# A four-stage block kernel on one core: lanes, PSUM banks and attention bursts regrouped

## The chip, the core and the metric

The kernel runs on one core of a Trainium2 chip. The metric is device time in microseconds (us) for one execution, from three runs; the profile is one further execution, taken by the hardware profiler. Engines are named as in the profile: PE (TensorE matmul), PEld (its weight load), DVE (VectorE), ACT (ScalarE), POOL (GpSimd), SP (SyncE, which issues the DMAs).

## What is computed

The input is x of 8 batches x 512 rows x 128 numbers, all float32. Four blocks follow each other, each with a residual:

```
x = x + gelu(linear_attention(layernorm(x)))        # 16 heads of 64: 1024 channels
x = x + fp4_ffn(layernorm(x))                       # 128 -> 352 -> 128, blocks of 16 quantised
x = x + causal_attention(layernorm(x))              # 16 heads of 8
x = x + experts(rmsnorm(layernorm(x)))              # 8 experts, best two, low-rank updates
```

The first block is per channel: with Q = elu(q)+1 and K = elu(k)+1,

```
KV = sum_s K*v;  Ksum = sum_s K;  out = (Q * KV / (Q*Ksum + 1e-6)) @ wo + bo
```

so each of the 1024 channels needs a reciprocal at each of 512 positions. The second block quantises its inputs, its weights and its middle to FP4 in groups of 16. The fourth computes both chosen experts of a token by masking the low-rank parts.

## The kernel before

Batches are independent. Each passes four functions: `linear_attention` (lines 650-698), `fp4_feed_forward` (747-791), `causal_attention` (794-929), then `routed` and `experts` (934-1058).

**The planner.** The functions issue nothing themselves. Each call becomes a `Step` of a `Plan` (129-307), with an engine, a cost (`cost`, 365-400) and the steps that it needs. `Plan.ordered` (221-297) replays all steps on five engines in its own time: at each moment an engine takes, among the steps that are ready and whose buffers are free, the one of lowest rank. `Plan.issue` (299-307) then emits them in that order, so every instruction of the main part has line 307 in the profile, and groups are told apart by tile names. On the chip each engine keeps that order and waits where an operand is late. Ranks come from `plan.span(lane, low, high)` (1061-1076), which spreads the steps of a function over an interval, in units of one batch. A lane hands out the places of a tag in the order of its own steps. `one_go` makes several calls one step.

**The lanes.** There are three: "front" runs linear attention of batch b at ranks b-1.0 to b-0.4 and the FP4 block at b-0.4 to b; "attention" runs at b to b+1; "experts" at b+1 to b+2.

**PSUM.** Eight banks: two `pair` tiles of two banks each for attention scores, one `mid` bank for the rest of attention, two `ahead` banks for the matmuls of the linear, FP4 and expert stages, and one `asum` bank for their accumulations (declared at 494-497; taken at lines 652, 776, 1036, 1046). `linear_attention` takes `asum` before its first chunk and holds it until its eighth.

**Linear attention**, eight chunks of 128 channels. A chunk has three 128x512 matmuls (q, k, v), five evictions by ACT, one DVE pass over q and k together (128x1024), two `scalar_tensor_tensor` for elu+1, one for K*v with its sum, one reciprocal of 128x512, one POOL product and one output matmul into `asum` (lines 653-686).

**Causal attention**, four groups of four heads. `spread` copies eight rows per head by nine DMAs into one of three K/Q tile pairs. `maxima` computes scores once for the row maxima (matmuls of 32 rows, four heads side by side on the array, then DVE `tensor_reduce`), and sends the maxima back by a DMA as a ninth row of Q. `scores` computes them again transposed, ACT takes the exponential, POOL masks the diagonal block. `weighed` multiplies by V, 32 columns per head, and `divided` normalises. Within a batch the maxima of group g+1 stand ahead of the scores of group g; nothing of batch b+1 is begun inside batch b.

Of the kernel before, what the change touches and what calls it, by code (L numbers as in the profile page):

```python
# [9 lines left out]
F32 = mybir.dt.float32  # L10
# [21 lines left out]
NFM = FM // P  # L32
NEG = -1.0e30
# [95 lines left out]
class Plan:  # L129
# [3 lines left out]
    HOP = {"tensor": 0.25, "vector": 0.12, "scalar": 0.12, "gpsimd": 0.15, "sync": 2.2}  # L133
# [38 lines left out]
    def one_go(self):  # L172
        return OneGo(self)

# [46 lines left out]
    def ordered(self):  # L221
# [25 lines left out]
        while done < len(self.steps):  # L247
            for e in self.engines:
                while busy[e] <= now:
# [19 lines left out]
                    s.start, s.end = now, now + s.cost  # L269
                    busy[e] = now + (0.06 if e == "sync" else s.cost)  # L270
# [54 lines left out]

class Span:
# [38 lines left out]
def cost(engine, method, out, ins, a, k):  # L365
# [3 lines left out]
    if engine == "tensor":  # L369
        if method == "transpose":  # L370
            return 0.14
        lhs, rhs = (list(a) + [k.get("lhsT"), k.get("rhs")])[1:3]
        rows, cols = lhs.shape[0], _free(lhs)
        n = _free(rhs)
        if BF16 in (getattr(lhs, "dtype", None), getattr(rhs, "dtype", None)):
            return 0.1
        if rows == 32:
            return 0.02 + n * 0.71e-3
        if cols == 32:
            return 0.02 + n * 0.8e-3  # L380
        return max(0.2, n * 1.667e-3)
    if engine == "vector":
        if method == "reciprocal":
            return 0.06 + n * 6.42e-3
        if method == "tensor_scalar":
            return 0.17 + n * 0.6e-3
        if method == "bn_stats":
            return 0.28
        return 0.15 + wide * 1.05e-3
    if engine == "scalar":  # L390
        return 0.25 + wide * 0.83e-3
    if engine == "gpsimd":
        if method == "affine_select":
            return 0.2 + n * 0.9e-3
        if method == "memset":
            return 0.15
        if k.get("op") == ALU.pow or ALU.pow in a:
            return 1.02
        return 0.12 + n * 2.25e-3
    return 2.0  # L400


LANES = ("front", "attention", "experts")
# [8 lines left out]
    ("xn", [P, NT, D], 2, F32),  # L412
    ("xnT", [P, S], 2, F32),
    ("two", [P, 2, S], 4, F32),
    ("v", [P, S], 2, F32),
    ("z", [P, S], 2, F32),
    ("wk_o", [P, D], 2, F32),
    ("half", [P, 512], 2, F32),
    ("sc", [P, 44], 4, F32),
    ("qa", [P, 704], 3, F32),  # L420
# [8 lines left out]
    ("oT", [P, NT, P], 1, F32),  # L429
    ("mx", [P, NT, 4], 3, F32),  # L430
    ("mr", [4, S], 1, F32),
# [12 lines left out]
    ("am", [P, 2, S], 1, F32),  # L444
# [4 lines left out]
def block_kernel(  # L449
# [46 lines left out]
    places("ahead", [P, 512], 2, pool=sums)  # L496
    places("asum", [P, 512], 1, pool=sums)
# [75 lines left out]
    va = const.tile([P, NT, H1, 32], F32, name="va", tag="va")  # L573
    dev.gpsimd.memset(va, 0.0)
    dev.gpsimd.memset(va[:, :, :, 8:9], 1.0)
# [8 lines left out]
    none = const.tile([4, S], F32, name="none", tag="none")  # L584
    dev.gpsimd.memset(none, 0.0)
# [5 lines left out]
    va = plan.fixed(va)  # L591
# [4 lines left out]
    one_go, new = plan.one_go, plan.tile  # L596
# [53 lines left out]
    def linear_attention(b):  # L650
        xnT = normed_T(xs[b], "ahead", "xn", "xnT")
        po = new("asum", [P, S])
        for c in range(NC0):
            cols = ts(c, P)

            ex = new("two", [P, 2, S])
            fm = new("two", [P, 2, S])
            v = new("v", [P, S])
            for i, w in enumerate((wq_sb, wk_sb, wv_sb)):
                pw = new("ahead", [P, S])  # L660
                nc.tensor.matmul(pw, w[:, cols], xnT, start=True, stop=True)
                if i == 2:
                    nc.scalar.activation(
                        v, pw, AF.Identity, bias=bqkv_sb[:, 2, c : c + 1]
                    )
                    break
                nc.scalar.activation(ex[:, i, :], pw, AF.Exp, bias=bqkv_sb[:, i, c : c + 1])
                nc.scalar.activation(
                    fm[:, i, :], pw, AF.Identity, bias=bqk1_sb[:, i, c : c + 1]
                )  # L670
            nc.vector.tensor_scalar(ex, ex, -1.0, 1.0, ALU.add, ALU.add)
            ks = new("s1", [P, 1])
            kv = new("s1", [P, 1])
            kf, qf = fm[:, 1, :], fm[:, 0, :]
            nc.vector.scalar_tensor_tensor(
                kf, ex[:, 1, :], 1.0, kf, ALU.min, ALU.max, accum_out=ks
            )
            nc.vector.scalar_tensor_tensor(qf, ex[:, 0, :], 1.0, qf, ALU.min, ALU.max)
# [3 lines left out]
            nc.vector.reciprocal(z, z)  # L682
            nc.gpsimd.tensor_tensor(z, qf, z, ALU.mult)
            wk_o = new("wk_o", [P, D])
            nc.scalar.activation(wk_o, wo_sb[:, c, :], AF.Copy, scale=kv)
            nc.tensor.matmul(po, wk_o, z, start=(c == 0), stop=(c == NC0 - 1))

        y = new("v", [P, S])
        nc.scalar.activation(y, po, AF.Identity, bias=bo_sb)
# [57 lines left out]
    def fp4_feed_forward(b):  # L747
        xn = new("xn", [P, NT, D])
        ln_apply(xn, xs[b], *ln_stats(xs[b]))
        xq = new("xn", [P, NT, D])  # L750
# [3 lines left out]
        xqT = new("xnT", [P, S])  # L754
        nc.scalar.copy(xqT, transposed(xq, NT, "ahead"))
        hqs = []
        for half in range(2):
            h = new("h", [P, 2, FF])
            for j in range(2):
                t = 2 * half + j  # L760
                pgu = [new("ahead", [P, FF]) for _ in range(2)]
                for i in range(2):
                    nc.tensor.matmul(
                        pgu[i], xqT[:, ts(t, P)],
                        wT[:, i].rearrange("p c m -> p (c m)")[:, 0:FF],
                        start=True, stop=True,
                    )
# [7 lines left out]
            hqs.append(hq)  # L775
        pd = new("asum", [P, NT, D])
        for t in range(NT):
            hqT = new("hqT", [P, NF0, P])
            nc.scalar.copy(
                hqT.rearrange("p c m -> p (c m)"),  # L780
                transposed(
                    hqs[t // 2][:, t % 2, :].rearrange("p (c m) -> p c m", c=NF0), NF0, "ahead"
                ),
            )
            with one_go():
                for c in range(NF0):
                    nc.tensor.matmul(
                        pd[:, t, :], hqT[:, c, :], wT[:, 2, c, :],
                        start=(c == 0), stop=(c == NF0 - 1),
                    )  # L790
        nc.vector.tensor_tensor(xs[b], pd, xs[b], ALU.add)


    def causal_attention(b):
# [7 lines left out]

        def spread(g):
            nc.sync.dma_start(qTs[g % NKT][8:P:32, :], none)
            for i, dst in enumerate((qTs[g % NKT], kTs[g % NKT])):
                for j in range(4):
                    nc.sync.dma_start(
                        dst[32 * j : 32 * j + 8, :],
                        qk[32 * g + 8 * j : 32 * g + 8 * j + 8, i, :],
                    )  # L810

        spread(0)
        spread(1)
        pv = new("mid", [P, S])
        with one_go():
# [5 lines left out]
            va.rearrange("p t h c -> p (t h) c")[:, :, 0:8],  # L821
            pv.rearrange("p (k c) -> p k c", c=8),
        )
        on = new("on", [P, NT, D])

        def largest(g, t, mx):

            n = (t + 1) * P
            pscs = [new("pair", [P, 2, 512]) for _ in range(2)]
            with one_go():  # L830
                for j in range(4):
                    rows = slice(32 * j, 32 * j + 32)
                    nc.tensor.matmul(
                        pscs[j // 2][:, j % 2, 0:n], qTs[g % NKT][rows, ts(t, P)],
                        kTs[g % NKT][rows, 0:n], start=True, stop=False,
# [6 lines left out]
            for i, psc in enumerate(pscs):  # L842
                nc.vector.tensor_reduce(
                    mx[:, t, 2 * i : 2 * i + 2], psc[:, :, 0:n], AX.X, ALU.max, negate=True
                )

        def to_queries(g, mx):

            pt = new("mid", [P, S])
            with one_go():  # L850
                for t in range(NT):
                    nc.tensor.transpose(pt[0:4, ts(t, P)], mx[:, t, :], ident)
            mr = new("mr", [4, S])
            nc.scalar.copy(mr, pt[0:4, :])
            nc.sync.dma_start(qTs[g % NKT][8:P:32, :], mr)

        def scores(g, t):

            n = S - t * P
            pscs = [new("pair", [P, 2, 512]) for _ in range(2)]  # L860
            with one_go():
                for j in range(4):
                    rows = slice(32 * j, 32 * j + 32)
                    nc.tensor.matmul(
                        pscs[j // 2][:, j % 2, 0:n], kTs[g % NKT][rows, ts(t, P)],
                        qTs[g % NKT][rows, t * P : S], start=True, stop=True,
                    )
            prs = []
            for psc in pscs:
                pr = new("pr", [P, 2, S])  # L870
                nc.scalar.activation(pr[:, :, 0:n], psc[:, :, 0:n], AF.Exp, scale=8.0 ** -0.5)

                nc.gpsimd.affine_select(
                    out=pr[:, :, 0:P], in_=pr[:, :, 0:P], pattern=[[0, 2], [1, P]],
                    compare_op=ALU.is_ge, fill=0.0, base=0, channel_multiplier=-1,
                )
                prs.append(pr)
            return prs

        def weighed(g, t, prs, po):  # L880
            with one_go():
                for j in range(4):
                    nc.tensor.matmul(
                        po[32 * j : 32 * j + 32, t * P : S], va[:, t, 4 * g + j, :],
                        prs[j // 2][:, j % 2, 0 : S - t * P],
                        start=(t == 0), stop=(t == NT - 1),
                    )

        def divided(g, po):
            oT = new("oT", [P, NT, P])  # L890
            nc.scalar.copy(oT.rearrange("p t q -> p (t q)"), po)
# [251 lines left out]
```

## Time and profile before

| what | value |
|---|---|
| runs | 1412.92, 1408.03, 1406.41 us; median 1408.03 us |
| profiled execution | 1418.83 us, of which the span of instructions is 1417.0 us |
| PE | busy 1185.3 us (84% of the span), granted clock 0.919 on average |
| DVE | busy 945.6 us (67%) |
| ACT | busy 699.3 us (49%) |
| POOL | busy 561.0 us (40%) |
| DMA | 15.11 MB in all, 6 tenths busy in the first fortieth of the span, below one tenth after |

The span is read in three parts. The first 263 us fill the lanes. From 263 to 1204 us the same pattern returns every 156 to 158 us, once a batch. The last 213 us empty the lanes. The page gives each engine's share in forty slices; a query over chosen stretches gives exact sums, and one over waits tells which engine's event ended an idle time. A float32 matmul that is no transpose leaves two records.

### The profile page before, as it was taken

The numbers are of one execution on the slowest core, as the hardware profiler recorded it, in microseconds if no ns is written. First come the engines' busy times: TensorE is split into PE (matmuls) and PEld (weight loads), VectorE is DVE, ScalarE is ACT, GpSimd is POOL, SyncE is SP. The second block draws the span as 40 slices with busy tenths as digits, with TensorE's granted clock in tenths as the row PEclk, the third lists the DMA queues.
The fourth block names the chain that finished last, engine by engine and source line by source line (L and its number), as shares of the span: only waits on it lengthen the run. The fifth ranks groups of instructions, "written<-read, shape, count | busy, mean of one in ns | idle before, by whom it ended". The sixth has DMA issues, their size and how long they took to land.

```text
span 1417.0 us, 17315 instructions
## 1 busy us (share of the span) xinstructions
PE 1185.3 (84%) x6185; PEld 535.4 (38%) x6185; DVE 945.6 (67%) x1717; ACT 699.3 (49%) x1244; POOL 561.0 (40%) x660
## 2 busy tenths in 40 slices
PE   2626779879998899989998899979998899699867
PEld 0203323433344334533354334433354335344333
DVE  5973894589676877498667976597749866352231
ACT  2632744474547464665547364656447453423321
POOL 3223212422663147423653156514652356244125
PEclk9965986999999899999999999999999999899879
DMA  6000000000000000000000000000000000000000
GB/s 181 0 0 1 12 1 5 2 12 1 5 16 7 7 5 1 17 12 1 6 16 11 2 5 2 9 12 5 2 9 12 1 5 9 6 7 13 1 0 8
DMA packets 18886, 15.11 MB, mean 11 GB/s; under 512 B 3632, under 2 KB 15344, under 8 KB 18800
## 3 DMA queue, kind: packets, MB, share of 16 engines
q1 hardware_dynamic: 18800, 14.01, 4.0%
q8 instruction: 49, 0.80, 0.2%
q14 instruction: 37, 0.30, 0.1%
HBM read 7.18 MB, written 2.10 MB: 7 GB/s over the span
## 4 chain that ended last, share of the span: by engine, by line
PE 47%; DVE 25%; POOL 9%; ACT 7%; issue 4%; POOLq 0%; ACTq 0%; DVEq 0%
PE ahead L307 19%; PE pair L307 13%; PE asum L307 8%; DVE z L307 6%; PE mid L307 6%; DVE mx L307 4%; DVE two L307 3%; DVE qa L307 3%; DVE sc L307 2%; POOL qa L307 2%; ACT pr L307 2%; POOL act L307 2%; POOL hq L307 1%; ACT two L307 1%; POOL z L307 1%
## 5 line engine op out<-in xcount | busy, mean ns | idle before, releaser
L307 DVE TENSOR_REDUCE mx<-pair 128x2 f32<-128x256 f32 (+3 forms) x256 | 198.7, 811 | 78.6 <-PE pair L307 77.8
L307 POOL TENSOR_TENSOR z<-two,z 128x512 f32<-128x512 f32 x64 | 86.4, 1350 | 346.0 <-DVE z L307 289.9
L307 ACT ACTIVATE pr<-pair 128x1024 f32<-128x1024 f32 (+3 forms) x256 | 168.5, 699 | 108.0 <-PE pair L307 103.5
L307 DVE RECIPROCAL z<-z 128x512 f32<-128x512 f32 x64 | 214.1, 3345 | 7.2 <-ACT z L307 7.2
L307 POOL TENSOR_SCALAR_AFFINE_SELECT pr<-pr 128x256 f32<-128x256 f32 x256 | 110.7, 446 | 120.9 <-ACT pr L307 119.4
L307 PE MATMUL pair<-kT,qT 32*128 32x128 f32 (+3 forms) x1024 | 131.6, 503 | 22.5 <-DVE mx L307 22.4
L307 POOL TENSOR_TENSOR act<-act,half 128x512 f32<-128x512 f32 x64 | 81.8, 1279 | 149.0 <-ACT half L307 90.0
L307 PE MATMUL pair<-qT,kT 32*128 32x512 f32 (+3 forms) x1024 | 130.3, 507 | 5.2 <-DVE mx L307 2.5
L307 PE MATMUL ahead<-um,b_sb 128*128 128x512 f32 x256 | 131.5, 614 | 2.9 <-DVE act L307 1.4
L307 ACT ACTIVATE two<-ahead,bqkv_sb 128x512 f32<-128x512 f32 x128 | 87.7, 686 | 59.0 <-PE ahead L307 57.7
L307 PE MATMUL asum<-z,wk_o 128*128 128x512 f32 x128 | 78.9, 702 | 42.6 <-POOL z L307 42.3
L307 PE MATMUL mid<-pr,va 128*32 128x512 f32 (+3 forms) x1024 | 107.5, 462 | 6.9 <-POOL pr L307 4.8
L307 DVE SCALAR_TENSOR_TENSOR two<-two,two 128x512 f32<-128x512 f32 x128 | 105.4, 845 | 3.7 <-DVE two L307 0.5
L307 ACT ACTIVATE two<-ahead,bqk_sb 128x512 f32<-128x512 f32 x128 | 85.7, 683 | 29.6 <-POOL z L307 16.6
L307 ACT ACTIVATE half<-ahead 128x512 f32<-128x512 f32 (+1 forms) x96 | 53.0, 553 | 82.4 <-PE ahead L307 80.5
L307 PEld LDWEIGHTS pair<-kT,qT 32*128 32x128 f32 x1024 | 53.2, 190 | 105.2 <-DVE mx L307 66.2
L307 PE MATMUL ahead<-xnT,wv_sb 128*128 128x512 f32 x128 | 76.5, 682 | 16.1 <-ACT two L307 15.3
L307 DVE SCALAR_TENSOR_TENSOR act<-act,ahead 128x512 f32<-128x512 f32 x64 | 43.3, 677 | 61.3 <-ACT act L307 61.3
L307 POOL TENSOR_TENSOR act<-act,tw 128x512 f32<-128x512 f32 x64 | 81.9, 1279 | 3.2
L307 PEld LDWEIGHTS pair<-qT,kT 32*128 32x128 f32 x1024 | 50.5, 192 | 81.4 <-ACT pr L307 38.3
L307 PE MATMUL ahead<-tT,w_sb 128*128 128x512 f32 x128 | 71.9, 644 | 7.6 <-ACT half L307 5.9
L307 PE MATMUL ahead<-xnT,wq_sb 128*128 128x512 f32 x128 | 72.3, 648 | 6.7 <-ACT half L307 3.4
(163 smaller groups left out, 1957.1 us busy)
## 6 DMA issues: line engine op xcount, KB each, us to landing
x<-in SPq DMA_DIRECT2D x8, 256.0 KB
qT<-qk SPq DMA_DIRECT2D x128, 16.0 KB
kT<-qk SPq DMA_DIRECT2D x128, 16.0 KB
out<-x SPq DMA_DIRECT2D x8, 256.0 KB
w_sb<-in SPq DMA_DIRECT2D x3, 256.0 KB
wq_sb<-in SPq DMA_DIRECT2D x1, 512.0 KB
wk_sb<-in SPq DMA_DIRECT2D x1, 512.0 KB
wv_sb<-in SPq DMA_DIRECT2D x1, 512.0 KB
```

The costliest lines, as they stand in the source:

```text
L307: getattr(e, method)(*a, **k)
```

## The change

1. **Four lanes.** "front" becomes "linear" (ranks b-1.5 to b-0.9) and "fp4" (b-0.9 to b-0.5), each with tiles of its own (`xf`, `xfT` for fp4). Attention of batch b runs at b to b+1, experts at b+1 to b+2, loads at b-2.0.
2. **Three `ahead` banks, no `asum`.** All accumulations take an `ahead` bank. The output projection of linear attention is done in two bursts of four matmuls, one after chunks 0-3 and one after chunks 4-7; the sum of the two goes through `y`. The same for the FP4 down projection and the experts' last matmuls, in two halves of two row tiles. `together` gives the first matmul of a burst the needs of all of them.
3. **Linear attention regrouped.** k, v, q instead of q, k, v; the 128x1024 pass becomes two of 128x512; the reciprocal two of 128x256; the POOL product is written into `qf`, of which there are six.
4. **Attention continued.** Groups are numbered 0 to 31 through all batches; `begin(n+1)` (projection and spread where a batch starts, then maxima) stands ahead of `attended(n)`, over the end of a batch too. V is held twice, at 16 columns per head instead of 32. The zeros that clear Q's ninth row are read from a Q tile instead of a tile of their own. The nine DMAs of a spread are one step.
5. **The planner's costs** are reset, as the third piece of the diff shows for matmuls: lower for the attention's narrow matmuls, nearly the same for the wide ones.

```diff
-LANES = ("front", "attention", "experts")
+LANES = ("linear", "fp4", "attention", "experts")
...
-    places("ahead", [P, 512], 2, pool=sums)
-    places("asum", [P, 512], 1, pool=sums)
+    places("ahead", [P, 512], 3, pool=sums)
...
+class Together:
...
+    def __exit__(self, *_):
+        some = self.plan.steps[self.first :]
+        for s in some[1:]:
+            for n in s.needs:
+                if n not in some:
+                    some[0].needs[n] = True
...
         if rows == 32:
-            return 0.02 + n * 0.71e-3
-        if cols == 32:
-            return 0.02 + n * 0.8e-3
-        return max(0.2, n * 1.667e-3)
+            return 0.068 + n * 0.38e-3
+        if cols < 64:
+            return 0.035 + n * 0.42e-3
+        return 0.03 + n * 1.62e-3
...
+        def feature(c, i, w, tag, **accum):
+            pw = new("ahead", [P, S])
+            nc.tensor.matmul(pw, w[:, ts(c, P)], xnT, start=True, stop=True)
+            ex, f = new("ex", [P, S]), new(tag, [P, S])
+            nc.scalar.activation(ex, pw, AF.Exp, bias=bqkv_sb[:, i, c : c + 1])
+            nc.scalar.activation(f, pw, AF.Identity, bias=bqk1_sb[:, i, c : c + 1])
+            nc.vector.tensor_scalar(ex, ex, -1.0, 1.0, ALU.add, ALU.add)
+            nc.vector.scalar_tensor_tensor(f, ex, 1.0, f, ALU.min, ALU.max, **accum)
+            return f
...
-            nc.vector.reciprocal(z, z)
-            nc.gpsimd.tensor_tensor(z, qf, z, ALU.mult)
+            for part in (slice(0, 256), slice(256, S)):
+                nc.vector.reciprocal(z[:, part], z[:, part])
+            nc.gpsimd.tensor_tensor(qf, qf, z, ALU.mult)
             wk_o = new("wk_o", [P, D])
             nc.scalar.activation(wk_o, wo_sb[:, c, :], AF.Copy, scale=kv)
-            nc.tensor.matmul(po, wk_o, z, start=(c == 0), stop=(c == NC0 - 1))
...
+        for half in range(2):
+            pairs = [products(c) for c in range(4 * half, 4 * half + 4)]
+            po = new("ahead", [P, S])
+            with together():
+                for i, (wk_o, qz) in enumerate(pairs):
+                    nc.tensor.matmul(po, wk_o, qz, start=(i == 0), stop=(i == 3))
+            if half == 0:
+                nc.scalar.activation(y, po, AF.Identity, bias=bo_sb)
+            else:
+                nc.vector.tensor_tensor(y, po, y, ALU.add)
...
+    def begin(n):
+        if n % NG == 0:
+            projected(n // NG)
+            spread(n)
+        if n % NG < NG - 1:
+            spread(n + 1)
+        maxima(n)
+
+    def causal_attention(b):
+        on = new("on", [P, NT, D])
+        for n in range(NG * b, NG * b + NG):
+            if n + 1 < NG * NB:
+                begin(n + 1)
+            attended(n, on)
+        to_model(b, on)
...
-        with plan.span("front", b - 1.0, b - 0.4):
+        with plan.span("linear", b - 1.5, b - 0.9):
             linear_attention(b)
...
-        with plan.span("front", b - 0.4, b):
+        with plan.span("fp4", b - 0.9, b - 0.5):
             fp4_feed_forward(b)
```

The changed program's order can be read without running it, and the prediction uses it. It has the same matmuls, 3689 in all and 460 per batch in mid-run. Before, the first and the last q/k/v matmul of a batch stand 222 matmuls apart on PE, the first and last of the FP4 block 127; after, 359 and 183. Ahead of the first matmul of attention stand 29 q/k/v matmuls before (24 belong to a batch) and 48 after. Behind the last one of the FP4 block stand 475 matmuls before and 574 after.

## The prediction

> **What bounds the kernel now.** I read the forty slices first, then busy sums over stretches cut where the slices change, then the chain and the waits of one batch.
>
> ```profile
> PE   2626779879998899989998899979998899699867
> DVE  5973894589676877498667976597749866352231
> PEclk9965986999999899999999999999999999899879
> ```
>
> PE and DVE swap roles: where DVE shows 8 or 9, PE drops to 6 to 8. The same by stretch (length, then busy us of each engine):
>
> ```profile
> core 0: us, PE busy (x) PEld busy (x) DVE busy (x) ACT busy (x) POOL busy (x), PEclk, DMA share, GB/s
> 0.00:142.00 142.00, 65.18 (x142) 28.12 (x143) 91.48 (x148) 50.70 (x90) 41.30 (x61) 0.77 0.15 45
> 142.00:263.00 121.00, 99.48 (x470) 39.94 (x468) 91.30 (x147) 60.33 (x106) 30.27 (x36) 0.84 0.03 5
> 602.00:655.00 53.00, 44.15 (x193) 20.09 (x191) 48.55 (x84) 27.71 (x49) 12.00 (x9) 0.90 0.05 9
> 655.00:759.00 104.00, 98.68 (x581) 45.41 (x580) 66.64 (x127) 58.16 (x106) 55.85 (x69) 0.97 0.03 8
> 1204.00:1240.00 36.00, 24.79 (x157) 13.70 (x156) 14.30 (x59) 14.70 (x28) 9.85 (x15) 0.82 0.03 6
> 1311.00:1346.00 35.00, 29.67 (x199) 11.59 (x196) 7.79 (x14) 12.74 (x20) 6.52 (x17) 0.80 0.00 1
> ```
>
> 602 to 759 is one batch in mid-run: 53 us in which DVE is 92% busy, then 104 us in which PE is 95% busy and DVE 64%. The chain names the first part's work: the reciprocal, and then what stands behind it.
>
> ```profile
> 605.06 3.26 DVE z L307
> 608.55 1.75 DVE two L307 x3
> 612.11 3.12 issue
> ```
>
> Busy PE is not dense PE, because a matmul's record lengthens when it is fed slowly. So I price work by rows without gaps. Elsewhere in the chain,
>
> ```profile
> 553.83 3.45 PE asum L307 x8
> ```
>
> is four 128x512 matmuls (two records each), 0.86 us each. Likewise, from the timeline at 691 to 705 us: four side-by-side score matmuls of 512, 384, 256, 128 columns 1.14, 0.93, 0.71, 0.50; four V matmuls 1.06, 0.85, 0.64, 0.42; four masks 0.40; a transpose 0.15; a two-pass 128-column matmul 0.22; 352 columns 0.60. Per batch: 68 wide ones 58.7, eight of 352 4.8, scores twice 26.2, masks 6.4, V 11.9, 76 transposes 11.4, 40 two-pass 8.6, the rest 1.0; sum **129 us of PE work**. By the same prices the 53 us hold 36.8 (0.69 per us), the 104 us 91.9 (0.88). DVE has 115 to 118 us per batch. Neither fills 157: the loss is that they are full in turn.
>
> **The change, part by part**, against the profiled execution (1418.83; span 1417.0).
>
> *Lanes and order.* Linear attention is the DVE-heavy part: per chunk 3.35 reciprocal, 0.78, two at 0.85, 0.71, 6.5 us, 52 per batch. Its q/k/v matmuls spread over 222 of a batch's 460 matmuls before, 359 after, so its DVE work lies beside more PE work. What holds it together before is the buffers: `asum` held for eight chunks, and both `ahead` banks held by the experts through two passes. What rate follows? An interpolation between the two stretches would say none is gained; but each is a limit of one engine, and in the middle neither need bind. Evidence from between: ten slices of 17.7 us have DVE at 82 to 90%; they hold 0.72 to 0.95, mean 0.83, several of them on the seam and at half clock. The best PE-bound stretches (503 to 602, 1126 to 1204) hold 0.91. I take the middle, 0.87: **129/0.87 = 148 us per batch** against 156; bounds 0.83 (155) and 0.92 (140).
>
> *What DVE is given.* Two 128x512 passes instead of one of 1024: 0.43 to 0.49 each against 0.78, +0.1 to +0.2, 1.2 per batch. Reciprocal in halves: rows of 44 and 512 elements (427 and 3345 ns) give 6.2 ns per element and 150 ns fixed, so 2 x 1.75 against 3.35, +0.15, 1.2 per batch. One sum for the second burst 0.69, two residuals in halves +0.3. Together +3.4.
>
> *POOL beside DVE.*
>
> ```profile
> L307 DVE SCALAR_TENSOR_TENSOR two<-two,two 128x512 f32<-128x512 f32 x128 | 105.4, 845 | 3.7 <-DVE two L307 0.5
> L307 DVE SCALAR_TENSOR_TENSOR act<-act,ahead 128x512 f32<-128x512 f32 x64 | 43.3, 677 | 61.3 <-ACT act L307 61.3
> ```
>
> The same operation of the same size takes 845 ns with two SBUF inputs and 677 with one from PSUM. The Trainium skill ("SBUF — State Buffer", Who interferes with whom) says why this speaks against the change: a DVE instruction with two SBUF inputs and a POOL one that reads SBUF exclude each other for the whole instruction. By that rule alone each of the five such DVE operations of a chunk (two passes, two elu, K*v) could wait up to a POOL product, 1.28 us: 40 x 1.28 = 51 us per batch, and DVE at 171 would be the bound. By the row the delay today is 0.17 on an elu, 0.10 on the pass, 0.03 on K*v, 3.7 us per batch, with POOL 23% busy in the DVE stretch; spread out it meets POOL's mean of 43%, so about 1.9 times that: +3.3. I take the row. DVE: 116.5+3.4+3.3 = 123 of 148, 83%: it fits.
>
> *The clock.* PE ran at 0.90 in the 53 us, though no wait of PE there exceeds 1.8 us. The skill's rule ("TensorE: Matmul & The Clock Gate", Why this matters for your kernels) is that idle gaps over about 3 us cost the full rate. By the rule nothing is recovered in this stretch; by the row 10% of 53, some 5 us per batch, could be. The 0.87 already has part of it; the rest goes into the range.
>
> *Attention over batch ends.* The 18 spread DMAs of a batch start go out on SP at 0.62 us each (timeline, 607 to 619 us), and the batch's first maxima wait for them. After, they are issued inside the previous batch. As nine in one step they hold SP for 5.6 us, and a DMA of maxima rows that is queued behind, with the scores of its group on PE, waits up to that; loads and stores too, but these have a batch of slack. Between 5.6 us lost per group and 3 gained per batch I take zero, because the maxima run a whole group ahead of the scores. V matmuls of 16 columns stream as many columns: cost zero, weight loads 109 ns beside PE. A zero row read from a Q tile: the same DMA.
>
> *Bursts.* Output matmuls keep number and price. Today PE waits 42.3 us in 26 waits for the POOL product:
>
> ```profile
> PE asum L307 <- POOL z L307: 42.3, 26, 4.6
> DVE x L307 <- PE asum L307: 78.6, 14, 9.1
> ```
>
> A burst waits for its latest input, and all of PE's queue stands behind it; the planner puts it late, so I count the wait at its present sum, between zero and three times that.
>
> *The ends.* In 0 to 142 us DVE is idle for 50 us, 35 of them between 71 and 142, while the FP4 block of batch 0 runs alone. After, 48 instead of 29 q/k/v matmuls stand ahead of the first attention, nearly all of batch 1, whose 52 us of DVE fill this; I take 26 saved (10 to 40). At the end, 1204 to 1240 holds 17.3 us of PE work in 36 and 1311 to 1346 20.3 in 35. After, attention 6 and experts 6 lie beside these parts (574 instead of 475 matmuls follow the last FP4 one); at 0.87 they would take 20 and 23: 28 saved, less a little, 24 (5 to 40). The last experts (1346 to 1417) stay alone.
>
> **Sum.** 263 to 1204 is 6.03 batches of 156: 6.03 x 8 = 48. 48+26+24 = 98; 1418.8-98 = 1321 for the profiled execution, which stood 1.0077 over the median: **1311 us**.
>
> **Rivals.**
> - *Only the ends gain.* The two engines interlock through PSUM (a bank is freed by ACT or DVE, the next matmul waits), the batch stays at 155 to 156. For it: still eight banks, and the seam slices' 0.83. Against it: 0.91 beside DVE at 65 to 67%. 1418.8-50-6 = 1363, median 1353; with half of that at the ends, 1380. Chance 0.24.
> - *Both fill.* 0.92 and ends at their best: 16 x 6.03+80 = 176, median 1233. Chance 0.08.
> - *Slower: PE stands at the bursts.* In the 16 projection bursts PE waits for the fourth pair, which hangs on DVE halves, ACT and a 1.35 us POOL product. Each wait costs itself, and the clock drops behind it. To eat 98 us beyond the 42 present, 16 bursts must wait 8.8 us each; at 12 us it is +52, median 1459. Against it: four pairs take DVE some 26 us and the planner sees that. Chance 0.12.
> - *The order does nothing:* on the chip other waits bring back the old pattern; within 0.5%, 1408. Chance 0.04.
>
> The forecast itself: 0.52. Faster by over 0.5% (about what a measurement of this kernel can tell from no change) 0.52+0.08+0.23 = 0.83; within it 0.05, one part of the first rival with the last; slower 0.12. The range runs from 1250 (0.91 in mid-run and ends near their best) to 1400, just inside the first rival's poor end.
>
> **What would show it.** A batch of 146 to 151 us in mid-run; DVE between 75 and 90% in nearly all slices between the sixth and the thirtieth, without a 9 beside a PE 7; the granted clock over 0.94 on average; attention of batch 0 begun with batch 1's q/k/v done; elu passes at 0.9 to 1.1 us (if they come to 1.5, the port rule was the right one); waits of PE for `qf` under 60 us in all. I am wrong if DVE's rows lengthen with POOL, or if PE's waits move from one end of the burst to the other.

## The result and the profile after

The changed kernel takes 1445.5 us (median; 1442.7 to 1450.6) against 1409.0 for the kernel before on the same chip: ratio 1.026, interval 1.022 to 1.030. It is slower; 1311 was foretold. Its profiled execution took 1450.6 us with a span of 1448.9 and a granted clock of 0.890 (before: 1418.8, 1417.0, 0.919). The main part's line is now L311.

The forty slices of the changed kernel:

```profile
PE   2545778978899799897997889898898889889967
DVE  5879878887856787875976769768975967234231
PEclk9767878989899899996998979999999879989978
```

The swap of roles that the prediction set out from is gone: no long 9 of DVE beside a PE 6 in mid-run. But PE has not become full. A few 7s, and 6s and 7s of the clock, are spread over the run. The same over stretches (columns as in the prediction's table; 585 to 754 us is one batch, 814 to 924 most of another):

```profile
0.00:142.00 142.00, 65.69 (x121) 25.23 (x121) 111.73 (x210) 61.70 (x112) 40.03 (x60) 0.79 0.15 45
142.00:261.00 119.00, 93.56 (x416) 46.34 (x417) 100.42 (x164) 58.97 (x109) 33.18 (x35) 0.81 0.03 5
...
585.00:754.00 169.00, 148.69 (x773) 68.60 (x772) 127.31 (x231) 86.07 (x155) 72.28 (x78) 0.90 0.03 7
...
814.00:867.00 53.00, 41.38 (x236) 18.35 (x229) 34.49 (x94) 22.73 (x45) 15.39 (x21) 0.77 0.06 15
867.00:924.00 57.00, 55.84 (x332) 24.43 (x331) 45.82 (x69) 34.94 (x65) 33.34 (x37) 1.00 0.01 2
```

In 814 to 867 no engine is full: PE 78%, DVE 65%, clock 0.77. Right behind it PE is 98% busy at full clock beside a DVE at 80%. So the two engines can be busy side by side; something else opens holes.

To set the two runs side by side I price each matmul as the prediction does, at the time that it takes without gaps, and note when the same amount of this dense PE work is done (116, 890 and all 1033 us of it). 116 to 890 are six batches, called mid-run from here on. The table has the length of each part in us; the foretold parts are rounded:

| | to 116 | 116 to 890 | per batch | rest | end |
|---|---|---|---|---|---|
| before | 263 | 936 | 156 | 218 | 1417 |
| after | 261 | 990 | 165 | 198 | 1449 |
| foretold | 237 | 888 | 148 | 194 | 1321 |

The 936 us hold 844.6 of busy PE and 91 of idle PE; the 990 hold 877.2 and 113. So of the 54 lost, 21 are longer waits, and 33 go to the *same matmuls taking longer*. The clock tells where: 68 us of the 936 ran at half clock (a granted clock of 0.50), 164 of the 990. In these stretches PE was busy for 141.5 us over 70.1 us of dense work (before: 64.8 over 35.2); in the rest of mid-run it was busy for 736.5 us over 703.9 (before: 779.4 over 739.0), which is less stretched than before.

Five of the waits of PE and DVE in the changed kernel (us in total, times, longest):

```profile
PE ahead L311 <- POOL qf L311: 24.3, 8, 5.4
PE pair L311 <- DMA kT<-qk: 22.4, 18, 6.9
DVE st linear L311 <- DMA x<-in: 21.9, 4, 6.7
PE mid L311 <- DVE on L311: 18.0, 7, 4.8
PE ahead L311 <- DVE act L311: 14.4, 6, 4.5
```

and before, where no wait of PE's matmuls for a `kT` DMA is listed, only two of its weight loads:

```profile
PEld pair L307 <- DMA kT<-qk: 1.5, 2, 0.8
DVE st front L307 <- DMA x<-in: 3.8, 1, 3.8
PE mid L307 <- DVE on L307: 5.3, 9, 1.1
PE ahead L307 <- DVE act L307: 1.9, 3, 0.9
```

The bursts (`qf`) are no trouble: 24 us against 42 before, of which mid-run has 1.1 against 19.6. Two of the other four name a DMA. The timeline at one of the three late x loads (start, length, engine, operation):

```profile
816.37 0.38 SPq L311 DMA_DIRECT2D out<-x  x1
...
817.63 0.54 SPq L311 DMA_DIRECT2D qT<-qT  x1
...
818.22 2.66 SPq L311 DMA_DIRECT2D qT<-qk  x4
...
820.92 2.63 SPq L311 DMA_DIRECT2D kT<-qk  x4
...
823.60 0.44 SPq L311 DMA_DIRECT2D x<-in  x1
826.35 0.68 DVE L311 BATCH_NORM_STATS2 st linear<-x 128x6 f32<-128x128 f32 x3 [5.01 <-DMA x<-in]
...
827.57 1.12 PE L311 MATMUL mid<-ident,on 128*128 128x128 f32 x4 [4.67 <-DVE on L311]
```

The x load takes one of five buffers, and has to wait for the store that sends the old content out. Between the two on SP stand the nine DMAs of a spread, 6 us of queue. DVE stands 5.0 us at the first instruction that needs it; `on`, next in DVE's order, does not need x at all, and PE waits 4.7 us for `on`.

What a short wait does to the clock, 20 us further on (first the wait, then the stretches cut at the clock's own edges):

```profile
848.86 0.33 PE L311 MATMUL ahead<-ident,xr 128*128 128x128 f32 x1 [1.80 <-ACT xr L311]
```

```profile
846.90:850.30 3.40, 1.59 (x15) 0.87 (x13) 1.87 (x4) 3.38 (x6) 0.81 (x2) 1.00 0.01 2
850.30:860.50 10.20, 10.20 (x47) 4.41 (x40) 5.67 (x30) 5.58 (x12) 2.62 (x5) 0.50 0.00 0
```

PE waits 1.8 us, is busy for 1.59 of 3.4 us, and then works 10.2 us without a gap at half clock. In the traces of before, after and run 18 all stretches at half clock are 3.4 us or multiples of it, but for the one that the end of the run cuts off. The kernel before has this wait for `xr` too, 1.75 us in five batches of its mid-run, with half clock right behind three of them.

### The profile page after: what moved, and what is told of

It is laid out like the page before. It is cut to its first block, busy times and chain, and to the rows that moved or that the text cites. A ratio compares the mean times of both kernels' runs of the same rounds, so it can differ in the third digit from the quotient of the medians.

```text
span 1448.9 us, 17554 instructions
## 1 busy us (share of the span) xinstructions
PE 1205.8 (83%) x6185; PEld 557.2 (38%) x6185; DVE 1013.5 (70%) x1869; ACT 692.5 (48%) x1244; POOL 581.1 (40%) x661
## 4 chain that ended last, share of the span: by engine, by line
PE 52%; DVE 29%; ACT 7%; SPq 3%; issue 3%; POOL 3%; DMA 2%; POOLq 0%; DVEq 0%; ACTq 0%
PE ahead L311 30%; PE pair L311 15%; DVE z L311 9%; PE mid L311 6%; DVE mx L311 3%; SPq L311 3%; DVE ex L311 3%; DVE qf L311 3%; DVE qa L311 2%; DVE kf L311 2%; DVE v L311 2%; DVE sc L311 2%; ACT pr L311 1%; POOL act L311 1%; DMA kT<-qk 1%
## 5 line engine op out<-in xcount | busy, mean ns | idle before, releaser
L311 DVE TENSOR_REDUCE mx<-pair 128x2 f32<-128x256 f32 (+3 forms) x256 | 199.2, 812 | 87.6 <-PE pair L311 87.2
L311 DVE RECIPROCAL z<-z 128x256 f32<-128x256 f32 x128 | 217.4, 1727 | 16.1 <-ACT z L311 16.0
L311 ACT ACTIVATE pr<-pair 128x1024 f32<-128x1024 f32 (+3 forms) x256 | 168.5, 701 | 86.2 <-PE pair L311 82.9
L311 POOL TENSOR_SCALAR_AFFINE_SELECT pr<-pr 128x256 f32<-128x256 f32 x256 | 121.6, 486 | 217.0 <-ACT pr L311 209.1
L311 PE MATMUL pair<-kT,qT 32*128 32x128 f32 (+3 forms) x1024 | 151.3, 528 | 46.2 <-DMA kT<-qk 22.4
L311 POOL TENSOR_TENSOR qf<-qf,z 128x512 f32<-128x512 f32 x64 | 86.1, 1346 | 187.1 <-DVE z L311 163.0
L311 PE MATMUL ahead<-um,b_sb 128*128 128x512 f32 x256 | 134.1, 622 | 13.6 <-DVE act L311 13.6
L311 PE MATMUL pair<-qT,kT 32*128 32x512 f32 (+3 forms) x1024 | 129.5, 515 | 13.4 <-DVE mx L311 9.1
L311 ACT ACTIVATE ex<-ahead,bqkv_sb 128x512 f32<-128x512 f32 x128 | 88.1, 689 | 92.4 <-PE ahead L311 78.4
L311 PEld LDWEIGHTS pair<-kT,qT 32*128 32x128 f32 x1024 | 61.8, 200 | 127.9 <-DVE mx L311 54.1
L311 POOL TENSOR_TENSOR act<-act,half 128x512 f32<-128x512 f32 x64 | 83.1, 1298 | 67.6 <-ACT half L311 43.7
L311 PE MATMUL mid<-pr,va 128*16 128x512 f32 (+3 forms) x1024 | 105.7, 466 | 4.2 <-POOL pr L311 3.6
L311 DVE TENSOR_SCALAR ex<-ex 128x512 f32<-128x512 f32 x128 | 79.2, 619 | 36.5 <-ACT ex L311 36.3
L311 PE MATMUL ahead<-qf,wk_o 128*128 128x512 f32 x128 | 75.8, 723 | 27.1 <-POOL qf L311 24.3
L311 POOL TENSOR_TENSOR act<-act,tw 128x512 f32<-128x512 f32 x64 | 86.9, 1358 | 3.8
L311 ACT ACTIVATE z<-qf,eps_sb,s 128x512 f32<-128x512 f32 x64 | 52.2, 816 | 74.7 <-DVE qf L311 74.6
L311 ACT ACTIVATE half<-ahead 128x512 f32<-128x512 f32 (+1 forms) x96 | 53.1, 553 | 71.5 <-PE ahead L311 68.1
L311 PEld LDWEIGHTS pair<-qT,kT 32*128 32x128 f32 x1024 | 50.0, 192 | 92.7 <-ACT pr L311 40.7
L311 PE MATMUL ahead<-xnT,wk_sb 128*128 128x512 f32 x128 | 79.4, 706 | 3.2 <-ACT kf L311 1.6
L311 DVE SCALAR_TENSOR_TENSOR act<-act,ahead 128x512 f32<-128x512 f32 x64 | 43.3, 679 | 53.7 <-ACT act L311 53.7
L311 DVE SCALAR_TENSOR_TENSOR v<-v,kf 128x512 f32<-128x512 f32 x64 | 62.3, 974 | 21.9 <-ACT v L311 21.4
L311 PE MATMUL ahead<-xnT,wq_sb 128*128 128x512 f32 x128 | 71.6, 642 | 5.4 <-ACT mk L311 2.0
```

The source lines that it names most:

```text
L311: getattr(e, method)(*a, **k)
```

## The experiments

Three theories. **A**: late x loads and slow spreads, since SP is one queue and the prediction took it as free. **B**: POOL lengthens DVE's rows. **C**: the planner's new costs give a bad order; lanes, halves or the continued attention are at fault. The rival to all is the prediction's own: PE and DVE interlock, and what delays DVE delays PE.

**1. x loads a batch earlier.** A sixth buffer; order of PE, DVE, ACT, POOL unchanged.

```diff
+            s.takes[0].place = self.own_x[n % 6]
...
+            order[i] = loads[n + 1] if 5 <= n < 7 else None
```

> The changed kernel with a sixth x buffer, handed out in turn, so that the load of batch 5, 6 and 7 is issued a batch earlier; the order of PE, DVE, ACT and POOL is the same, instruction by instruction. Theory A (late transfers: DVE stands 5 us at 486, 653 and 824 us for an x load that SP issues behind a store and nine spread DMAs, PE stands with it, and the half clock that follows halves 30 to 50 us of work): the three waits go, the stretches 478-513, 655-690 and 814-867 come back from 0.5 to about 0.8 of dense PE work per us, and 25 to 50 us go, 1395 to 1420. Theory B (DVE is lengthened by POOL's port): 1440 to 1450, nothing but the 15 us of direct waiting can move, and most of that is taken up by the next DVE work.

1426.4 us (ratio to before 1.012, 1.009 to 1.014): 19 gained, less than the 25 to 50 of theory A. The three waits for x are gone, DVE's rows are as they were, the batch falls from 165 to 162. So late x loads are real, and a part.

**2. POOL with an eighth of its reads beside DVE.** The 128x512 products are made on the last 64 columns only; two fills with a constant stand in for the rest, so part of the computation is left out.

```diff
+                    e.memset(a[0][:, 0:448], 0.5)   # twice
+                    a[:3] = [x[:, 448:S] for x in a[:3]]
```

> The changed kernel, but POOL's products of 128x512 (linear attention, swish, token weight) are made on the last 64 columns only, and two memsets of the first 448 stand before it: nearly the same POOL time, seven eighths less reading of SBUF; this leaves work out. Same order on all engines. Theory B (port): the elu and K*v rows fall from 0.85-0.97 to about 0.70, the 128x512 pass from 0.62 to about 0.45, DVE busy falls by 50 us, and the time by 30 us or more (to 1415 or below). Theory A (late transfers): the rows fall too, but the time stays within 10 us of 1445, as the holes are elsewhere.

1419.3 (1.006, 1.004 to 1.008): 26 gained. In the changed kernel the groups had (busy us, mean ns)

```profile
L311 DVE TENSOR_SCALAR ex<-ex 128x512 f32<-128x512 f32 x128 | 79.2, 619 | 36.5 <-ACT ex L311 36.3
L311 DVE SCALAR_TENSOR_TENSOR v<-v,kf 128x512 f32<-128x512 f32 x64 | 62.3, 974 | 21.9 <-ACT v L311 21.4
L311 DVE SCALAR_TENSOR_TENSOR qf<-ex,qf 128x512 f32<-128x512 f32 x64 | 62.2, 971 | 4.3 <-ACT qf L311 0.3
```

and with an eighth of the POOL reads

```profile
L316 DVE TENSOR_SCALAR ex<-ex 128x512 f32<-128x512 f32 x128 | 67.7, 529 | 34.6 <-ACT ex L316 34.2
L316 DVE SCALAR_TENSOR_TENSOR v<-v,kf 128x512 f32<-128x512 f32 x64 | 52.2, 815 | 22.0 <-ACT v L316 21.6
...
L316 DVE SCALAR_TENSOR_TENSOR qf<-ex,qf 128x512 f32<-128x512 f32 x64 | 46.9, 733 | 7.7 <-ACT qf L316 4.1
```

But of the 26, 12 lie in the first 261 us and some 14 in six batches; B is true and small in mid-run. Time at half clock there did not fall with it (198 us against 164).

**3, 4. The planner's costs.** The old costs again (with the spread as nine steps), and alone a price for a DMA on SP:

```diff
-    return 0.06
+    return 0.65
```

> The changed kernel with the planner's costs of before (matmuls, evictions, DMA 2.0 us and a hop of 2.2) and the nine DMAs of a spread as nine steps; everything else changed. Theory C (the reset costs make an order that the chip does not keep, above all a DMA counted at 2.3 us from start to use instead of 4.2): clearly faster than 1445, 1380 to 1420. If the costs are not at fault: 1440 or slower.

> The changed kernel with one number of the planner changed: a DMA holds SP for 0.65 us, as the profile shows, instead of 0.06; a spread of nine then takes 5.85+2.0. Theory A and C: waits for spreads and loads fall from 44 us (22 on DVE, 22 on PE) to under 15, and the time to 1400-1430. Theory B: within 10 us of 1445.

Old costs: 1461.7 (1.037, 1.034 to 1.039), 16 slower; C in this form falls. (In this profile the six batches are 10 us shorter than in the changed kernel, and the end is 15 us longer.) With 0.65 us per DMA: 1414.6 (1.004, 1.003 to 1.006), 31 faster, the x waits of mid-run gone and PE's waits for `kT` down from 22.4 to 12.9 us. A planner that knows of SP's queue goes around it; but the whole order moves with the costs, so this run alone does not say which wait made the difference.

**5. Runs 1 and 2 together.**

> The x loads a batch earlier and the POOL products on 64 of 512 columns (the rest of each product is filled with a constant ahead of it, so part of the computation is left out), in the same order of PE, DVE, ACT and POOL as the changed kernel. If the late x loads (19 us) and the longer DVE rows (26 us) are two separate losses, the time is 1445.5 - 19 - 26 = 1400, within 8. If they cost the same time once (DVE late, whatever made it late), it is about 1419. Prediction's step 1 wants 148 us per batch in mid-run once both are gone; the rival (an interlock of PE with the other engines) wants 155 or more.

1402.8 (0.991, 0.989 to 0.994; single runs from 1387 to 1411): within that scatter A and B add up. The batch is still 159 us, not 148.

**6. DVE relieved.** Reciprocals on 32 of 256 columns, which leaves most of them out.

```diff
+                if method == "reciprocal" and _free(a[0]) == 256:
+                    a[:2] = [x[:, 0:32] for x in a[:2]]
```

> Each half reciprocal works on 32 of its 256 columns, in the unchanged order, so most reciprocals are left out: DVE has some 16 x 1.45 = 23 us less per batch, about 185 in all. If DVE's being late is what stretches the batch (the bound shared with PE, DVE at 78 per cent), the mid-run period falls from 165 to 148 or less, the start by another 20, and the time to about 1300. If PE is held by waits that do not come from DVE's work (DMA, bursts behind POOL, its own banks), the mid-run stays above 158 and the time above 1380.

1392.7 (0.988, 0.984 to 0.992): 53 faster, where 145 was expected if DVE's lateness stretches the batch. 32 of it is in the start (261 to 229 us), which DVE does bound; the batch stays at 161, with 97 us of idle PE and 150 at half clock in mid-run. There DVE's load is not what holds PE, so neither an interlock through DVE's work nor "full in turn" explains the batch. An interlock through the banks that ACT frees was not run.

**7. Attention apart.** A batch's attention begins with the batch.

```diff
+        begin(NG * b)
         for n in range(NG * b, NG * b + NG):
-            if n + 1 < NG * NB:
+            if n % NG < NG - 1:
```

> Attention of a batch begins only with the batch (its projections, both spreads and first maxima inside its own span), everything else as changed. The prediction counted the continuation at zero, between 3 us per batch gained and 5.6 lost per group. If the continuation is what makes the x loads late and holds PE at the joins, this one is faster than the changed kernel by 15 to 25: 1420 to 1430. If it does what it was priced at best, slower by up to 24: 1470. At zero: 1440 to 1450.

1470.7 (1.042, 1.039 to 1.046), 25 slower. Of the 20 us between the two profiles 13 lie in the start, where the first batch's attention begins later, and 6 in mid-run: the continuation gains about 1 us per batch there. It is not at fault.

**8. Costs as measured**: 0.65 per DMA, six x buffers, DVE's rows at 0.61 and 0.89 us.

```diff
-        return 0.15 + wide * 1.07e-3
+        return 0.15 + wide * (1.07e-3 if from_sums else 1.45e-3)
```

> The planner counts 0.65 us of SP per DMA, has six x buffers, and counts DVE's passes and two-SBUF operations at 0.61 and 0.89 us for 512 columns, as the changed kernel's rows have them; everything is computed. If wrong costs in the planner are what makes its order bad, this is below the run with the 0.65 alone (1414.6) by some 10 to 20, 1395 to 1405, and below before (1409). If the order matters little beyond the late loads, it is 1410 to 1420.

1412.4 (1.000, 0.999 to 1.001): no better than run 4. Neither true DVE costs nor a sixth buffer bring anything further.

**9. Fillers, first try.** Useless matmuls ahead of the transposes of `xr` and `on`.

```diff
+                    e.matmul(s.takes[0].place, self.fill[0], self.fill[1], start=True, stop=True)
```

> The changed kernel in its own order, with matmuls of no use put where PE stands idle: two 128x512 ones (1.7 us) ahead of the transposes of xr in the four batches where a wait of 1.8 us stands there and 27.3 us at half clock follow, five (4.3 us) ahead of the transposes of on in the three batches with a wait of 4.7 us and 20.5 us at half clock behind it. The waits themselves stay as long. If the half clock behind short waits is what the time is lost to, these 48 us of half clock go and the time falls by up to 24, to about 1422. If the clock costs nothing because the other engines set the pace, it stays at 1445. If the fillers hold up the work behind them, it is longer, up to 1465.

1457.7 (1.033, 1.030 to 1.035). A miss of the design: the filler at `on` writes the one `mid` bank, which `on` itself still reads, so it waited 4.6 to 4.8 us too and then ran for 7.0 to 7.2 us behind that, three times. At `xr` it sat right, but the sum says nothing.

**10, 12. The continuation alone, in the kernel before**; in 12 each spread is one step, too, and the planner counts 0.65 us of SP per DMA.

```diff
-            causal_attention(b)
+            causal_attention(b - 1)   # with begin(n + 1) ahead of attended(n)
```

> The kernel before with one part of the change alone: attention continued across batches (with V in 16 columns and two V tiles); lanes, banks, bursts, reciprocals and planner costs stay as before. From the run with attention apart (25 us slower than the changed kernel) the continuation is worth 25: 1385. By the prediction's estimate it is worth nothing: 1409. If it brings late x loads here too, 1415 to 1430.

> The kernel before with attention continued across batches, each spread one step of nine DMAs, and a planner that counts 0.65 us of SP for every DMA and 2.0 us for its landing. If queueing on SP is what an order has to know of, this is faster than the continuation alone by 5 to 15: 1370 to 1380. If the kernel before has no such queue, the same: 1385.

1578.7 (1.119, 1.116 to 1.122) and 1538.2 (1.090, 1.087 to 1.093): far off every theory. Run 10 against the kernel before:

```profile
PE ahead L308 <- POOL hq L308: 63.5, 14, 8.0
PE asum L308 <- POOL z L308: 61.3, 39, 4.6
```

```profile
PE ahead L307 <- POOL hq L307: 14.5, 13, 6.6
```

Attention of batch b+1 now stands in the queues inside batch b, while its FP4 block is still due at the end of batch b: PE waits for `hq` in every batch. The added 49 us of this wait are a part of the 168 only; time at half clock in mid-run is 243 us against 68. That the continuation needs the front due half a batch earlier, as the change has it, fits this but was not run alone.

**11. Reciprocals whole.**

```diff
-            for part in (slice(0, 256), slice(256, S)):
-                nc.vector.reciprocal(z[:, part], z[:, part])
+            nc.vector.reciprocal(z, z)
```

> The changed kernel with the reciprocals whole again, 3.35 us in place of 2 x 1.73. By the prediction's working 0.15 us less of DVE per chunk, 10 us in all, of which a start bound by DVE gets 3 and the mid-run little: 1436 to 1443. If the halves let maxima and act passes in between, and PE waits for those, this one is slower: 1450 to 1460.

1443.8 (1.023, 1.020 to 1.026): the halves make no difference that can be told.

**13. Fillers where the bank is free**: at `xr`, and ahead of a batch's first maxima, which wait for the spread's DMA.

> The changed kernel in its own order with useless matmuls of 128x512 (0.86 us each) where PE stands idle and the bank is free: two ahead of the xr transposes in four batches (waits of 1.8 us, 27 us at half clock behind them), and two, at one batch start seven, ahead of the first maxima of a batch in six batches (waits of 1.5 to 6.9 us for the spread's DMA, 34 us at half clock behind them). 21.5 us of useless work in waits of 22 us. If the half clock costs the time, 61 us of it go and the time falls by 20 to 30, to 1416 to 1425. If the clock only goes with waits that other engines set, 1440 to 1450.

1432.8 (1.016, 1.014 to 1.019): 13 us faster with 21 us *more* work on PE. Time at half clock in mid-run falls from 164 to 123 us. It is less than the 20 to 30 expected, but nothing that PE waits for was made faster, so this part is the clock's alone: half clock behind a wait costs time, and does not only go with it. A part of this is old: the wait for `xr` stands in the kernel before as well.

**14. A spread of five DMAs.** q and k lie side by side in one tile, so a DMA carries both.

```diff
-            for i, dst in enumerate((qTs[n % NKT], kTs[n % NKT])):
-                for j in range(4):
-                    nc.sync.dma_start(dst[32 * j : 32 * j + 8, :], qk[... , i, :])
+            for j in range(4):
+                nc.sync.dma_start(qks[n % NKT][32 * j : 32 * j + 8, :, :], qk[... , :, :])
```

> The changed kernel with q and k rows of a group side by side in one tile, so that a spread is five DMAs of up to 8 partitions x 2 x 512 in place of nine; everything else as changed. If SP's 0.62 us per DMA is the term that failed, a spread holds SP for 3.1 us in place of 5.6: the late x loads come 2.5 us earlier (three times), and the first maxima of a batch up to 5 us earlier (eight times, with half clock behind each): 1420 to 1430. If a DMA's price goes by its bytes, nothing changes: 1445.

1409.6 (0.999, 0.998 to 1.000): 36 faster, more than the theory had. The planner ordered parts of the run differently there; run 17 takes this apart.

**15. One lane for linear attention and FP4.**

```diff
-        with plan.span("fp4", b - 0.9, b - 0.5):
+        with plan.span("linear", b - 0.9, b - 0.5):
```

> FP4 and linear attention take their PSUM banks in one lane's turn again; due times, three banks, bursts and the rest as changed. If the four lanes are what lets short steps come between and break the chains, 1420 to 1430; if they gain what they were priced for, slower, 1460 to 1480; if the lanes matter little because the due times already order the work, 1440 to 1450.

1513.8 (1.074, 1.071 to 1.076), 68 slower: with these due times and three shared banks the fourth lane is needed. It is no loss.

**16. Runs 8 and 14 joined.**

> The kernel with 0.65 us per DMA, six x buffers and DVE costs as measured (1412.4), with the spread of five DMAs. The lanes, bursts, banks, halves and the continued attention are all in it. If the spread's DMAs still hold PE at batch starts there, 1395 to 1405, faster than before (1409 to 1411). If the planner already goes around them, the same: 1412.

1423.2 (1.009, 1.007 to 1.011): a miss, slower than either. Another plan came out, and what made it worse was not settled. Plans of almost equal inputs differ by some 10 us here (1412.4 and 1423.2), which is why the next two keep the order.

**17. Five DMAs in the changed kernel's own order.** The plan is made with nine, five are issued.

```diff
+            if getattr(s, "four", None):
+                calls = calls[:1] + [("dma_start", v, {}) for v in s.four]
```

> The changed kernel's order to the instruction on PE, ACT, DVE and POOL; only that each spread is five DMAs on SP in place of nine. If SP's queue is the failed term, most of the 36 us of the run before it stay: 1410 to 1425. If the other order made them, 1435 to 1445.

1410.1 (1.001, 0.999 to 1.003): 35 us gained with nothing moved on PE, DVE, ACT or POOL. SP's queue at a late x load:

```profile
795.92 0.38 SPq L314 DMA_DIRECT2D out<-x  x1
797.29 0.54 SPq L314 DMA_DIRECT2D qkT<-qkT  x1
797.88 2.66 SPq L314 DMA_DIRECT2D qkT<-qk  x4
800.64 0.38 SPq L314 DMA_DIRECT2D x<-in  x1
```

```profile
DVE st linear L314 <- DMA x<-in: 15.4, 4, 7.5
PE pair L314 <- DMA qkT<-qk: 8.5, 10, 4.6
```

Four DMAs take 2.66 us whether they carry 16 KB each, as in the changed kernel, or 32 KB: here the price is per DMA. x is issued 4.7 us after the store instead of 7.2, and of the 15.4 us 7.5 are the start's: the three late loads cost 2.5 to 2.7 us each instead of 5. PE's waits for the spread fall from 22.4 to 8.5. A batch takes 160 us, time at half clock in mid-run falls from 164 to 137.

**18. All three**: run 17, x loads as in run 1, fillers at `xr`.

> As the run with five DMAs in the changed order, and x loads a batch earlier in a sixth buffer, and two useless 128x512 matmuls ahead of the xr transposes in the four batches with a wait there. If late loads, spread and half clock are separate losses, 1445 less 19, less 10 to 20 for the spread without its part in the late loads, less 6: 1400 to 1410, no slower than before. If they are one loss seen three times, 1415 to 1425.

1395.0 (0.989, 0.988 to 0.991): 50 us below the changed kernel and 1.1% below the kernel before, with everything computed. The two stretches at the same `xr` as above, filled:

```profile
804.70:808.10 3.40, 3.35 (x20) 1.72 (x16) 1.81 (x3) 3.40 (x7) 0.50 (x2) 1.00 0.01 2
808.10:818.30 10.20, 9.52 (x80) 4.15 (x81) 7.99 (x34) 8.69 (x19) 3.72 (x8) 1.00 0.03 6
```

The clock stays at 1.00, and the second stretch, just as long, holds 8.9 us of dense PE work where the changed kernel's holds 5.0. 92 us of mid-run are at half clock, and a batch takes 157 us when the useless matmuls are not counted as work: no less than the 156 before. By the profiles start, mid-run and end take 257, 940 and 193 us against 263, 936 and 218 before, so what is gained over the kernel before lies at the two ends.

## Why the prediction was wrong

- **Attention over batch ends: the term put at nothing that failed.** The nine DMAs were seen, priced at 5.6 us of SP and then taken at zero, for two reasons. One, "the maxima run a whole group ahead of the scores", is beside the point at a batch start, where spread and first maxima follow each other at once. The other, "loads and stores too, but these have a batch of slack", does not hold: an x load waits for the store that frees its buffer, and behind it comes the spread. Run 17 puts four of the nine DMAs at 35 us; the other five still stand in the queue. The continuation itself was rightly taken at about nothing: 1 us per batch in mid-run (run 7), where the text had 3 at best.
- **The rate in mid-run: the other step that failed, by 17 us per batch.** 0.87 was read off slices as if it followed from how DVE's work is spread; 129 us of work in 165 are 0.78. DVE's load came out as foretold, 122.7 us per batch (736.5 in mid-run), but PE's idle time rose from 91 to 113 us. Run 6 shows that DVE's load was not the limit. What the runs do show: short waits at fixed places in the order, each passed on to PE because an engine keeps its order (DVE's 5.0 us for x became PE's 4.7), and the clock behind them. With the queue shortened, the loads early and the clock kept up at four waits (run 18), the batch is 157 us, a rate of 0.82: still not 148, and not below the 156 before. So of the 8 us per batch that spreading DVE's work was to bring nothing is seen even then. Why stays open; the waits for `mx`, and for `act` at 4.5 us three times, were not tried.
- **The clock: the term mis-sized, and in sign.** The row had it (0.90 with no wait over 1.8 us); the text counted a recovery. Instead half clock in mid-run went from 68 to 164 us and the mean over the run from 0.919 to 0.890. The rule of the Trainium skill weighed there ("TensorE: Matmul & The Clock Gate", Why this matters for your kernels), no idle gap over about 3 us, is too mild here: waits of 1.75 us before the change and 1.8 us after it are followed by 3.4 us and up to 10.2 us at half clock. The trace decides. New waits were to be priced with the half clock behind them.
- **The start: 2 us instead of 26.** The reasoning that batch 1's chunks would fill DVE's idle time took DVE's work as it was. DVE is busy 182 us of the first 262 before and 213 after, when 19 chunks instead of 16 are through their reciprocals, and its rows are longer. It bounds much of this stretch: runs 2 and 6 take 12 and 32 us off it.
- **POOL beside DVE: right.** 3.3 us per batch were to be added to some 3.7; run 2 takes 53.6 us of DVE work away (1013.5 to 959.9), 6.7 per batch. The elu rows, 0.85 and 0.97, lie about where they were foretold, far from the 1.5 of the bare rule. What was missed: at the start, where DVE bounds, it costs 12 us. One slip: the two passes have one SBUF input, so the rule as told there does not cover them; their row moved all the same, from 619 to 529 ns in run 2.
- **Bursts: right** (24 us of waits, under 60), so the rival that ended slower had the right side and the wrong mechanism, and its 1459, close to 1445, is luck: PE does not stand at bursts. **The end: right**, 20 for 24. **Halves**: right, run 11.
- The rival "only the ends gain" had mid-run closer (155 to 156), but none of the cases held a *new* wait on a queue, and so none came near 1445 by its own mechanism.

## What to carry to other kernels

When steps move, list for each queue what now stands behind them, SP's too, and ask of each load what frees its buffer and when: "a batch of slack" is a number to look up. Price a short wait of PE at its length plus the half clock behind it, and look for it in the clock row before trusting a rate. Moving work between stages did not help here, where PE waits at fixed points of its order; experiments on an unchanged order tell these losses apart, where a planner's new plan shifts the time by some 10 us by itself.

## What the hardware showed

- SP takes 0.66 us per DMA of eight partitions (2.66 us for four), the same at 16 KB and 32 KB; five instead of nine per spread were worth 35 us.
- The clock changes in steps of 3.4 us. In the changed kernel's trace 31 of its 39 falls to half follow a step in which PE was busy for at most 51% (as the 1.59 of 3.40 us above), the other eight one of 58 to 90%, and no step busy for less than 49% kept the full clock. Twice it stayed at half for three steps in which PE was busy without a gap. Useless matmuls in the wait keep it up (runs 13 and 18).
- A POOL product does block a DVE instruction that meets it: the pass that began at 816.27 us, 0.12 us into a product of 1.27 us, took 1.44 us where 0.43 to 0.61 is usual. The mean stays low because most do not meet one: 109 of 320 such instructions overlap a product, and the passes among them take 0.82 us on average, the others 0.53.
